# A three-stage decoder layer on one core: both norms' moments on ScalarE, two context products on VectorE

## The chip, the cores and the metric

The kernel runs on one core of a Trainium2 chip. The metric is the device time of one launch in microseconds (us). In what follows PE is TensorE (its weight loads are listed apart, as PEld), DVE is VectorE, ACT is ScalarE, POOL is GpSimd and SP is SyncE.

## The reference

A post-norm decoder layer works on `x` of 16 sequences of 256 tokens with 512 channels. Each of its three parts is added to its input and followed by a norm without parameters.

```python
def reference(x, ctx_2048, w_q, w_k, w_v, w_o, ssm_kernel, D, gamma, W):
    x = _layernorm(x + attention(x, w_q, w_k, w_v, w_o))       # 16 heads, causal, ternary weights
    x = _layernorm(x + _xattn(ctx_2048, ctx_2048, x, ssm_kernel, D, 8))
    x = _layernorm(x + _ffn(x, gamma, W))
    return x

def _layernorm(x, eps=1e-05):
    return (x - mean(x)) / sqrt(var(x) + eps)                  # over the 512 channels

def _xattn(k, v, q, ssm_kernel, D, head_dim):                  # 32 heads of 8 rows, length 512
    kv = einsum('bhil,bhjl->bijhl', k, v)                      # products of rows i and j
    y = causal_convolution(kv, ssm_kernel)                     # along l, by FFT
    return einsum('bijhl,bhil->bjhl', y + kv * D, q)

def _ffn(x, gamma, W):
    xn = x * rsqrt(mean(x * x) + 1e-6) * gamma
    a = 127 / (max(abs(xn)) + 1e-5)                            # 8-bit rounding per token
    return einsum('bsd,od->bso', clip(round(xn * a), -128, 127) / a, ternary(W))
```

Since the context is both `k` and `v`, the product of rows i and j is that of j and i. The second norm's output is fed to the feed-forward part, whose sum is normed a third time.

## The kernel before

The attention stage fills the first half of the time and leaves its normed result transposed in SBUF (`x1t`). The change lies in the second stage, which goes over the 32 heads of the convolution layer; one head is one 128-token tile of the output (8 rows times 16 sequences), so a head carries the convolution, both norms and the feed-forward part of those tokens. The heads are pipelined: step `h` of the loop does the convolution of head `h`, the second norm of head `h-1`, the feed-forward product of head `h-2`, and the third norm's output of head `h-3`. An instruction's place in each engine's queue is the place of its call in the loop, since all five engines are scheduled by hand.

For a head, `kv` (128 x 4 blocks x 576) holds the context products: five groups of columns, by the distance 0 to 4 between the two rows multiplied. The squares (distance 0) come from ACT (L760), the groups 1, 2 and 3 (512 elements per partition each) and 4 (256 elements) from POOL (L754, `multiply`). The convolution is a matrix product with a Toeplitz tile `w`: `multiplied` (L785) makes block `lb` of 4 from `lb+1` blocks of `kv` into `y`, of which there are two buffers in PSUM. In the profile, blocks 0, 1, 2 and 3 show up as 4, 8, 12 and 16 matmuls; they are called y0 to y3 below.

`with_queries` (L797, L800, L803, L809, L812, all DVE) multiplies `y` by the queries `q` into `own` and `turn`; its last instruction, L812, frees the `y` buffer. `add` (POOL, L960, and L962 for blocks 1 to 3) sums them, and `read` (PE, L820) transposes and accumulates them into `tok`, 128 tokens by 512 channels. `tok` is complete when block 3 of the head has been read, which happens in the next step.

The second norm: `second_moments` takes the mean and variance of `tok` (DVE bn_stats L835, bn_aggr L837, and quarters of the variance for two roots, L840), ACT takes the root (L845), DVE its reciprocal (L851), ACT a Newton step (L855), DVE the reciprocal of that (L863). `second_centred` (L878) makes `xn`, `second_max` (L882) its maximum, and `second_norm` the normed rows `x2` (ACT, L888), the small scales (DVE, L890 to L895) and the rounded activations `fq_t` and `fq_i` (ACT, L897 and L188). SP transposes these by DMA, PE multiplies (L907, `acc_f`), and `feed_forward` makes `r3 = acc_f * inv + x2` (DVE, L911) and the third norm's moments, again by L835, L837 and L840. `finish` writes the result a step later (ACT L926, then a DMA). `copy` (ACT, L772 and L773) fetches the next head's queries from `x1t`.

After the loop, `last_heads` finishes the last three heads; nothing is left there to overlap with, and its instructions keep the order of the calls. The last head's activations are transposed by PE and copied by ACT (`fit`, L196).

Four lines of the first stage are used later for comparison: L158 (DVE) compares weights, with two inputs in SBUF; L132 (ACT) sums absolute weights with the accumulator; L182 scales activations (there on POOL) and L251 (POOL) builds a diagonal.

## Time and profile before

| | us |
|---|---|
| median of 3 runs (lowest to highest) | 863.07 (862.62 to 864.34) |
| the profiled execution, its whole time | 861.76 |
| its span, first to last instruction | 860.0 |
| busy in the span: PE / DVE / ACT / POOL | 803.8 / 690.5 / 427.0 / 583.4 |
| busy in one step of the second stage, 682.08 to 694.48 (12.40 us): PE / DVE / ACT / POOL | 12.25 / 10.85 / 5.22 / 11.52 |

The profile is of one execution, 1.3 us under the median. The second stage begins at about 441 us with the first L785 and its steady steps end at about 841 us. All times of instructions below are us from the start of the span.

### The profile page before, as it was taken

The numbers are of one execution on the slowest core, as the hardware profiler recorded it, in microseconds if no ns is written. First come the engines' busy times: TensorE is split into PE (matmuls) and PEld (weight loads), VectorE is DVE, ScalarE is ACT, GpSimd is POOL, SyncE is SP. The second block draws the span as 40 slices with busy tenths as digits, with TensorE's granted clock in tenths as the row PEclk, the third lists the DMA queues.
The fourth block names the chain that finished last, engine by engine and source line by source line (L and its number), as shares of the span: only waits on it lengthen the run. The fifth ranks groups of instructions, "written<-read, shape, count | busy, mean of one in ns | idle before, by whom it ended". The sixth has DMA issues, their size and how long they took to land.

```text
span 860.0 us, 20228 instructions
## 1 busy us (share of the span) xinstructions
PE 803.8 (93%) x7754; PEld 555.9 (65%) x7754; DVE 690.5 (80%) x1889; ACT 427.0 (50%) x707; POOL 583.4 (68%) x652
## 2 busy tenths in 40 slices
PE   4889999999999999998878999999999999999993
PEld 3556666666666666665646767776777677777762
DVE  6757887788888778876666888988898889888885
ACT  6555655556565555655644334433443444344434
POOL 5265544545454454544639999999999999999980
PEclk9999999999999999999979999999999999999997
DMA  9111222333122222211320233223323332333211
GB/s 319 45 33 53 66 69 69 75 76 76 26 63 68 71 75 76 51 39 35 88 65 19 69 99 95 71 81 99 88 67 91 99 84 68 95 98 74 75 38 55
DMA packets 102207, 64.51 MB, mean 75 GB/s; under 512 B 66464, under 2 KB 83104, under 8 KB 102112
## 3 DMA queue, kind: packets, MB, share of 16 engines
q1 hardware_dynamic: 102112, 63.23, 27.5%
q8 instruction: 61, 1.00, 0.5%
q14 instruction: 34, 0.28, 0.1%
HBM read 43.34 MB, written 8.47 MB: 60 GB/s over the span
## 4 chain that ended last, share of the span: by engine, by line
PE 77%; DVE 10%; ACT 6%; issue 4%; POOL 2%; DMA 0%; ACTq 0%; DVEq 0%; POOLq 0%
PE y L785 32%; PE s L341 6%; PE acc L293 6%; PE s L381 5%; ACT p L386 4%; PE tok L820 4%; PE pv L409 4%; PE s L334 4%; PE acc_o L482 3%; DVE nmax L346 3%; PE acc_f L907 3%; PE sums L416 2%; PE s L374 2%; PE acc_v L311 2%; PE tp L528 1%
## 5 line engine op out<-in xcount | busy, mean ns | idle before, releaser
L785 PE MATMUL y<-kv,w 128*128 128x288 f32 x1280 | 335.0, 409 | 4.4 <-DVE turn L812 2.0
L785 PEld LDWEIGHTS y<-kv,w 128*128 128x128 f32 x1280 | 234.0, 191 | 64.9 <-PE tok L820 10.5
L960 POOL TENSOR_TENSOR own<-own,turn 128x512 f32<-128x512 f32 x127 | 161.7, 1274 | 21.1 <-DVE turn L812 11.0
L390 POOL TENSOR_SCALAR_AFFINE_SELECT p<-p 128x512 f32<-128x512 f32 x128 | 81.3, 659 | 139.5 <-ACT p L386 129.1
L754 POOL TENSOR_TENSOR kv<-c 128x512 f32<-128x512 f32 (+1 forms) x128 | 144.4, 1140 | 2.9 <-PE sums L416 2.9
L346 DVE TENSOR_REDUCE nmax<-s 128x4 f32<-128x512 f32 (+1 forms) x128 | 116.5, 952 | 35.5 <-PE s L341 35.5
L386 ACT ACTIVATE p<-s 128x1536 f32<-128x1536 f32 x64 | 92.9, 1452 | 70.3 <-PE s L381 70.2
L845 ACT ACTIVATE root<-quarter 128x3 f32<-128x3 f32 (+2 forms) x34 | 7.0, 204 | 159.5 <-DVE quarter L840 159.5
L396 POOL TENSOR_TENSOR both<-p 128x512 f32<-128x512 f32 x64 | 82.3, 1286 | 5.3
L797 DVE SCALAR_TENSOR_TENSOR own<-y,q 128x128 f32<-128x128 f32 x128 | 36.7, 286 | 50.5 <-PE y L785 42.6
L962 POOL TENSOR_TENSOR own<-own 128x256 f32<-128x256 f32 x95 | 69.1, 727 | 7.5
L293 PE MATMUL acc<-xit,w 128*128 128x256 bf16 x504 | 68.9, 276 | 3.6 <-DVE w L158 3.4
L800 DVE TENSOR_TENSOR own<-y,q 128x384 f32<-128x384 f32 x128 | 70.1, 548 | 0.0
L803 DVE TENSOR_TENSOR turn<-y,q 128x384 f32<-128x384 f32 x128 | 70.1, 548 | 0.0
L820 PEld LDWEIGHTS tok<-ident,own 128*128 128x128 f32 x318 | 37.7, 141 | 38.5 <-POOL own L962 26.0
L293 PEld LDWEIGHTS <-w 128*128 128x128 bf16 x512 | 45.9, 99 | 24.1 <-issue 8.5
L820 PE MATMUL tok<-ident,own 128*128 128x128 f32 x318 | 58.7, 283 | 2.4 <-issue 1.2
L341 PE MATMUL s<-kt,qt 32*128 32x128 f32 (+1 forms) x1024 | 60.0, 348 | 0.0
L381 PE MATMUL s<-qt,kt 32*128 32x256 f32 (+1 forms) x1024 | 57.4, 335 | 0.0
L409 PE MATMUL pv<-p,va 128*32 128x256 f32 (+1 forms) x1024 | 54.9, 332 | 0.0
L421 ACT COPY ot<-pv 128x256 f32<-128x256 f32 x64 | 23.9, 373 | 50.8 <-PE pv L409 50.2
L334 PE MATMUL s<-mask,ident_h 128*128 128x256 bf16 x256 | 38.3, 271 | 11.0 <-ACT p L386 9.9
(148 smaller groups left out, 1359.8 us busy)
## 6 DMA issues: line engine op xcount, KB each, us to landing
xt<-in_x SPq DMA_DIRECT2D x16, 512.0 KB, 4.1
xr<-in_x SPq DMA_DIRECT2D x16, 512.0 KB, 4.6
c<-in_ctx_t SPq DMA_DIRECT2D x32, 256.0 KB, 3.3
w<-taps SPq DMA_DIRECT2D x32, 256.0 KB, 4.1
out_y<-res SPq DMA_DIRECT2D x31, 256.0 KB, 2.3
c<-in_ctx_t SPq DMA_DIRECT2D x32, 128.0 KB, 3.2
x1t<-in_w_q SPq DMA_DIRECT2D x1, 1024.0 KB, 6.6
x1t<-in_w_k SPq DMA_DIRECT2D x1, 1024.0 KB, 9.4
```

The lines of the kernel that those rows point to most:

```text
L293: nc.tensor.matmul(acc[:, j, :], w[:, c, o * P : (o + 1) * P], m.xit[:, c].rearrange("p t k -> p (t k)"), start=(c == 0), stop=(c == NB - 1),)
L341: nc.tensor.matmul(s[:, r, lo:hi], m.qt[rows, g, q0 : q0 + P], m.kt[rows, g, 0:nk], start=False, stop=True, skip_group_check=True,)
L346: nc.vector.tensor_reduce(m.nmax[:, t, :, g], s[:, :, cols], AX.X, ALU.max, negate=True)
L381: nc.tensor.matmul(s[:, r, lo:hi], m.kt[rows, g, k0 : k0 + P], m.qt[rows, g, q0:S], start=False, stop=True, skip_group_check=True,)
L386: nc.scalar.activation(p, s[:, :, 0 : 3 * P], AF.Exp)
L390: nc.gpsimd.affine_select(out=own, in_=own, compare_op=ALU.is_ge, fill=0.0, base=0, pattern=[[0, 4], [1, P]], channel_multiplier=-1,)
L396: nc.gpsimd.tensor_tensor(both, p[:, :, P : 2 * P], p[:, :, 2 * P : 3 * P], ALU.add)
L409: nc.tensor.matmul(acc[rows, q0:S], m.va[:, j, 4 * g + r, :], p[:, r, src], start=(j == 0), stop=(j == 1), skip_group_check=True, tile_pos ...
L754: nc.gpsimd.tensor_tensor(kv[:, :, at : at + n * B].rearrange("p c (i b) -> p c i b", b=B), c[:, :, i : i + n, :], c[:, :, i + d : i + d + ...
L785: nc.tensor.matmul(y[:, Y0 + k * HALF : Y0 + (k + 1) * HALF], lhs, kv[:, mb, k * HALF : (k + 1) * HALF], start=(mb == 0), stop=(mb == lb),)
L820: nc.tensor.matmul(tok[:, lb, :], lhsT=own[:, d, :], rhs=ident, is_transpose=True, start=(d == last), stop=(d == 0))
L960: nc.gpsimd.tensor_tensor(own[:, 0:4, :], own[:, 0:4, :], turns[lb], ALU.add)
```

## The change

Four things are edited.

1. `moments2` takes the moments on ACT, for both the second and the third norm. One ACTIVATE Copy over 512 elements gives the sum by its accumulator, a small one scales it to minus the mean, an ACTIVATE Square with that as its bias gives the sum of squared deviations, and small ones (two for the second norm, one for the third) make the quarters. Their wide output goes to a tile that nobody reads.
2. The products of distance 3 and 4 move from POOL to DVE, to other places of the loop: distance 3 in front of `second_centred`, distance 4 between `copy` and `feed_forward`. For the first head, POOL still makes them, distance 4 now after distance 3.
3. `second_max` is called ahead of the Newton step instead of after it (in the loop only).
4. `x2` is made after `fq_i` instead of ahead of the small scales. The sign of the mean is flipped where it is used.

```diff
+        unused = pb.tile([P, E], BF16, name="unused")
...
-            def multiply(k):
-                part(k * P, XD, 0, k)
-                if k == 2:
-                    part(4 * P, 4, 0, 4)
+            def multiply(k, engine):
+                part(k * P, 4 if k == 4 else XD, 0, k, engine)
...
         def moments2(src, roots, forms):
-            st = sm.tile([P, 6], F32, name="st2")
-            nc.vector.bn_stats(st, src)
-            mv = sm.tile([P, 2], F32, name="mv2")
-            nc.vector.bn_aggr(mv, st)
+            total = sm.tile([P, 1], F32, name="total2")
+            nc.scalar.activation(unused, src, AF.Copy, accum_out=total)
+            minus_mean = sm.tile([P, 1], F32, name="minus_mean")
+            nc.scalar.activation(minus_mean, total, AF.Copy, scale=-1.0 / E)
+            squares = sm.tile([P, 1], F32, name="squares")
+            nc.scalar.activation(unused, src, AF.Square, bias=minus_mean, accum_out=squares)
             for i in forms:
                 a, b = FORMS[i]
-                nc.vector.tensor_scalar(roots.quarter[:, i : i + 1], mv[:, 1:2], a / 4, b / 4, ALU.mult, ALU.add)
-            return mv[:, 0:1]
+                nc.scalar.activation(
+                    roots.quarter[:, i : i + 1], squares, AF.Copy, scale=a / (4 * E), bias=b / 4
+                )
+            return minus_mean
...
         def second_norm(m, roots):
...
-            m.x2 = fp.tile([P, E], F32, name="x2")
-            nc.scalar.activation(m.x2, m.flat, AF.Identity, bias=shift, scale=rstd)
...
             m.fi = rounded(fp, "fq", m.ft)
+            m.x2 = fp.tile([P, E], F32, name="x2")
+            nc.scalar.activation(m.x2, m.flat, AF.Identity, bias=shift, scale=rstd)
...
             multiply(first_head, 3)
+            multiply(first_head, 4)
...
+                on(multiply, h + 1, 3, nc.vector)
                 on(second_centred, h - 1)
+                on(second_max, h - 1)
                 if h > 0:
                     newton(roots)
-                on(second_max, h - 1)
...
-                on(multiply, h + 1, 3)
                 on(second_norm, h - 1, roots)
                 on(turn, h - 1)
                 on(finish, h - 3, roots, h - 3)
                 on(copy, h + 1)
+                on(multiply, h + 1, 4, nc.vector)
                 on(feed_forward, h - 2, ahead)
```

More of the change, by code (lines that the diff above doesn't have):

```diff
@@ L751, in prepare, with part @@
             kv = cp.tile([P, NB, NPAIR], F32, name="kv")
-            def part(at, n, i, d):
-                nc.gpsimd.tensor_tensor(
+            def part(at, n, i, d, engine):
+                engine.tensor_tensor(
                     kv[:, :, at : at + n * B].rearrange("p c (i b) -> p c i b", b=B),
@@ L866, in shifted @@
             shift = sm.tile([P, 1], F32, name="shift")
-            nc.vector.tensor_scalar(shift, mean, res, -1.0, ALU.mult, ALU.mult)
+            nc.vector.tensor_scalar(shift, mean, res, None, ALU.mult)
             return shift
@@ L877, in second_centred @@
             m.xn = fp.tile([P, E], F32, name="xn")
-            nc.vector.scalar_tensor_tensor(m.xn, m.flat, m.mean, gam, ALU.subtract, ALU.mult)
+            nc.vector.scalar_tensor_tensor(m.xn, m.flat, m.mean, gam, ALU.add, ALU.mult)
         def second_max(m):
@@ L940, in square, with multiply @@
             m.inputs[5]()
-        def multiply(m, k):
-            m.inputs[3](k)
+        def multiply(m, k, engine=nc.gpsimd):
+            m.inputs[3](k, engine)
         def copy(m, *blocks):
```

## The prediction

> **What bounds the kernel now.** The page comes first: PE is busy 803.8 of 860.0 us, and the only lines touched by the change run in the second stage. The table of windows for one of its steps, 682.08 to 694.48, has PE busy 12.25 of 12.40 us, POOL 11.52, DVE 10.85, ACT 5.22. Three engines look full, so shares decide nothing; the chain of waits in order of time does. One step of it:

> ```profile
> 682.08 2.18 PE y L785 x8
> 684.26 0.39 PE tok L820 x2
> 684.65 2.91 PE y L785 x12
> 687.57 0.86 PE acc_f L907 x4
> 688.43 0.44 PE tok L820 x4
> 688.87 3.90 PE y L785 x16
> ...
> 692.86 0.29 DVE own L797
> 693.15 0.47 DVE own L800
> ...
> 694.35 0.14 issue
> 694.48 2.18 PE y L785 x8
> ```

> The same picture repeats every 12.40 us (y1 starts at 632.48, 644.88, 657.28 and so on). The loop is: y3 ends at 692.76; 0.10 later DVE starts on it and needs 1.48 to free the buffer; 0.15 later PE starts y1, 1.72 after the end of y3; then 2.18 + 0.39 + 2.91 + 0.86 + 0.44 + 3.90 = 10.68 bring the next y3. 1.72 + 10.68 = 12.40. Two terms hold a stall: y1 takes 2.18 and not 8 x 0.243 = 1.94, since its weight load comes after the wait, and the pair of tok reads takes 0.39 and not 0.22, since it waits for POOL's sum of block 3, which itself starts 0.15 after DVE's L812.

> What DVE and POOL do just before that is in the timeline:

> ```profile
> 690.53 1.28 POOL L754 TENSOR_TENSOR kv<-c 128x512 f32<-128x512 f32 x1
> 690.75 0.74 DVE L911 SCALAR_TENSOR_TENSOR r<-acc_f,inv,x 128x512 f32<-128x512 f32 x1
> 691.53 0.69 DVE L835 BATCH_NORM_STATS2 st<-r 128x6 f32<-128x512 f32 x1
> 691.75 1.28 POOL L960 TENSOR_TENSOR own<-own,turn 128x512 f32<-128x512 f32 x1
> 692.86 0.29 DVE L797 SCALAR_TENSOR_TENSOR own<-y,q 128x128 f32<-128x128 f32 x1 [0.23 <-PE y L785]
> ```

> Whether DVE is ever late for y3 is in the list of waits (484 to 840 us; who waited for whom, in total, times, longest). L797 is the one that waits:

> ```profile
> DVE own L797 <- PE y L785: 35.3, 55, 1.0
> ```

> DVE has 0.23 us to spare before y3 and POOL 0.64 before its sum of block 3. So relieving either moves nothing in the loop; making DVE late by more than its slack costs each step the difference.

> **Part by part, in the loop.** *DVE, removed:* second moments 685.77 to 686.84, 1.07 us; third moments 691.53 to 692.62, 1.09. *DVE, added:* two tensor_tensor. L800 (384 elements) takes 548 ns and L809 (64) 215, so 1.04 ns an element: 0.68 for distance 3 (data phase 0.53) and 0.42 for distance 4 (0.27). Net 1.06 less. *POOL, removed:* 1.28 + 0.73 (L754's two forms) = 2.01 us.

> *The wait that is added.* These two are the first DVE instructions of this stage with both inputs in SBUF; all others with two tensor inputs read one of them from PSUM. The first stage shows what such an instruction does beside POOL:

> ```profile
> L158 DVE SCALAR_TENSOR_TENSOR w<-x1t,limits x2: 1285/1437/1589, 11.5 to 17.0; 128x1024 bf16<-128x1024 f32 x2
> L251 POOL TENSOR_SCALAR diag<-ident,x_v x4: 602/616/1562, 7.8 to 19.0; 128x128 f32<-128x128 f32 x4
> ```

> Alone it took 1285 ns. At 16.95 it found POOL's L182 running until 17.48, and took 1589: 0.53 of waiting and then 1.06 of data. The POOL instruction queued behind it took 1562 instead of 616. So I take it that DVE waits for the end of the running POOL instruction, runs its data phase, and POOL's next one waits for that. [...]

> Distance 3: issued at 685.77 behind block 1, it finds POOL's L960 (685.35 to 686.62), and ends at 686.62 + 0.53 = 687.15 or so. Behind it on DVE queue xn, its maximum, the reciprocal L851 and block 2; who waits for these are ACT's Newton step, POOL's sum of block 2 and the `y` buffer of the next y0. xn 687.1 to 687.8, maximum to 688.55, L851 at 688.47, block 2 from 688.56 instead of 688.22 to 690.04. The buffer is wanted at 692.76, so 2.7 us cover that. POOL, held until 687.17, ends distance 2 at 688.3, the sum of block 1 at 690.3, and the first half of the sum of block 2 (L960) at 691.55, where before it only began at 691.75.

> Distance 4: before, r3 was issued 1.14 after L863; now L863 is at 689.96, so distance 4 is issued at 691.10, waits for L960 until 691.55, and ends at 691.83; r3 ends at 692.49. y3 is due at 692.86: slack 0.37 instead of 0.23. PE's y0 (692.98) now waits for this product too, with 1.1 us to spare. So the loop is not touched: 0.

> *ACT, added per step.* Rows: 128x512 with constants 0.63 (L188), with one pointer 0.71 (L897), ACTIVATION_READ_ACCUMULATOR 190 ns (L132), of which 0.10 overlaps, a small one 0.20 (L845), a dependent step 0.03. Sum, minus mean, squares and a quarter: 0.63 + 0.09 + 0.03 + 0.20 + 0.03 + 0.71 + 0.09 + 0.03 + 0.20 = 2.01, a second quarter 0.10: 4.1 a step, 9.3 busy of 12.40. Its order: fq_t at 690.98, fq_i, x2, result, both copies to 694.56, third moments, squares to 697.0. tok is complete at 697.05, so the second moments start at once at 697.10, and the root ends at 699.44, which in the step shown is 687.04. DVE asks for it at 688.47. Slack 1.4 us, cost 0; the minus mean (685.65) is there before xn (687.1). The copies end 0.9 later than before, so DVE's L800 of block 0 starts near 694.60 instead of 694.45; DVE then idles 1.04 before y1's result, so 0. SP's transpose goes 0.2 later (its product is 7 us away) and the output DMA 0.9 later, with it the next head's loads, wanted two steps on. 0. x2 is read a step later, 0. Swapping the maximum and the Newton step is within the slack just used.

> A second price on ACT is excluded by the trace: L760 (Square) and the copies already alternate with the root, and ACT_TABLE_LOAD occurs once in this stage (1283 ns, at 464.49). [...]

> **At the ends.** Start: in step h=1, PE's read of block 2 stood 0.81 us for POOL (471.23), behind an L754 of distance 3 that goes; that step took 12.70 against 12.40, so -0.3. The first head's reordered products end at 437.9 on POOL, y0 begins at 441.30: 0.

> The tail is in the open, and here the moments are a chain:

> ```profile
> 849.15 0.80 ACT L926 ACTIVATE res<-r,shift,res 128x512 f32<-128x512 f32 x1
> 849.94 0.59 ACT L196 COPY fit<-tp 128x512 bf16<-128x512 bf16 x1
> 850.58 1.89 PE L907 MATMUL acc_f<-w,fit 128*128 128x512 bf16 x4 [0.68 <-ACT fit L196]
> 853.30 0.69 DVE L835 BATCH_NORM_STATS2 st<-r 128x6 f32<-128x512 f32 x1
> 854.43 0.20 ACT L845 ACTIVATE root<-quarter 128x1 f32<-128x1 f32 x1 [1.89 <-DVE quarter L840]
> ```

> (a) Last head's second moments: tok complete at 843.73; root ended at 845.16, now 843.77 + 2.01 + 0.10 + 0.23 = 846.11. DVE's L851 had waited behind xn, so the Newton step ends 0.66 later (847.30); fq_t no longer waits for x2 and starts at 848.37 instead of 847.87: +0.50, fq_i ends at 849.75. (b) The copy of `fit` stands in ACT's queue behind the early result and behind `feed_forward` of the head before, whose moments are now ACT's too, and x2 is there as well: x2 849.66 to 850.44, result to 851.15, moments 851.06 to 853.07, copy at 852.98 instead of 849.94: +3.04, which contains (a). (c) The last third moments: r3's end to root's end 853.26 to 854.63 = 1.37, now 0.03 + 2.01 + 0.23 = 2.27: +0.9. Tail: +3.9.

> Sum: 0 - 0.3 + 3.9 = +3.6. The profiled execution's 861.76 becomes 865.4; it lies 1.3 under the median, so 863.07 becomes 866.7. Unknown sizes: each of the six accumulator reads on the tail's path may hide wholly or not at all (0 to 0.19, near the row's 0.09: together -0.5 to +0.6); ACT and DVE read tok together in the tail (a collision is in no row: 0 to one xn, 0.74; I take 0). The case alone: 865 to 868.5.

> **Rivals.**

> *Distance 4 misses its gap.* If it is issued after 691.55, it meets POOL's second half, L962 (to 692.4), ends at 692.64, r3 at 693.30, and block 3 is 0.44 late. In 29 steps +12.8 with the tail +16.4: 879.5. It decides from 0.45 us of extra delay on DVE between L812 and r3. [...] Against: the measured wait of L158 was exact to 0.01. Chance 0.12.

> *PE gains from the relief.* With POOL 2 us freer the pair of tok reads might lose its 0.17 stall and y1 its 0.24: 0.41 x 29 = -11.9, with the ends 854.8. For it: PE's reads waited 23.4 us for L962 by the list of waits. Against: both hang on L812, which comes 1.58 after y3 whatever DVE did before. Chance 0.08.

> *A cheap tail.* If the moments of the last-but-one head don't hold up the copy of `fit`, only (a) and (c) remain: +1.1, 864.2. Against: the queue keeps the order of the calls. Chance 0.12.

> **How the numbers follow.** The forecast has 0.68. About 0.2% (1.7 us) can be told from no change: faster is the second rival, 0.08; same is the third and a sliver of the forecast, 0.13; slower the rest, 0.79. The range, 863.0 to 871.0, holds forecast and cheap tail and a mild form of the first rival (a delay of up to 0.15 a step, 4.4 us), and leaves out the strong form and the second rival.

> **What would show it.** Right: steps still of 12.40; DVE idle before L797 of block 3 of about 0.4; L754 on DVE longer than 0.68 by the wait (near 1.4 for distance 3, 0.87 for distance 4); POOL idle for over 2 us a step; `fit` copied 11.4 us after the last y3 instead of 8.4. Wrong: steps of another length, or L797 of block 3 waiting for r3 instead of y3.

## The result, and the profile after

The changed kernel takes 866.65 us (median of 19 runs, 864.78 to 869.7) against 863.74 (861.15 to 865.81) for the kernel before on the same chip. The ratio is 1.0042 with a 95% interval of 1.003 to 1.0053: slower by 3.6 us (2.6 to 4.6), more than the 0.2% that can be told from no change. (The two medians are 2.9 apart, the means of the 19 runs 3.6.) The forecast was 866.7 and slower.

The page shows work that moved, with nothing gained where it counts. ACT has 121.5 us more than before (427.0), POOL 43.6 less (583.4), DVE 1.7 more (690.5):

```profile
PE 799.2 (92%) x7754; PEld 558.8 (65%) x7754; DVE 692.2 (80%) x1727; ACT 548.5 (63%) x1123; POOL 539.8 (62%) x590
```

The line numbers have shifted: the `y` matmul is L784 now, the five lines of `block` L796 to L811, the reads of `tok` L819, the products L755, POOL's two sums L964 and L966, r3 L915. The chain of waits in order of time, for PE's part of one step (start, length, engine and line):

```profile
695.39 2.18 PE y L784 x8
697.57 0.39 PE tok L819 x2
697.96 2.91 PE y L784 x12
700.87 0.88 PE acc_f L911 x4
...
707.79 2.18 PE y L784 x8
```

From y1 to y1 it is 707.79 - 695.39 = 12.40, as before, and the two stalls are still there: y1 takes 2.18, the pair of reads 0.39. Measured from one end of y3 to the next, the 29 steps from h=2 on take 12.39 to 12.40 in both kernels, but for one of 12.45 before, and the step h=1 takes 12.40 now and took 12.70.

The timeline of the same stretch has the two new products on DVE, and POOL around them (start, length, engine and line; in brackets the idle time before it and what ended that):

```profile
695.39 1.28 POOL L964 TENSOR_TENSOR own<-own,turn 128x512 f32<-128x512 f32 x1 [2.04 <-DVE turn L811]
...
698.65 1.27 POOL L964 TENSOR_TENSOR own<-own,turn 128x512 f32<-128x512 f32 x1
699.08 1.39 DVE L755 TENSOR_TENSOR kv<-c 128x512 f32<-128x512 f32 x1
699.88 1.73 POOL L755 TENSOR_TENSOR kv<-c 128x512 f32<-128x512 f32 x1
700.09 0.20 ACT L849 ACTIVATE root<-quarter 128x3 f32<-128x3 f32 x1
701.77 0.16 DVE L855 RECIPROCAL inv_root<-root 128x3 f32<-128x3 f32 x1
703.59 1.27 POOL L964 TENSOR_TENSOR own<-own,turn 128x512 f32<-128x512 f32 x1
704.36 0.79 DVE L755 TENSOR_TENSOR kv<-c 128x256 f32<-128x256 f32 x1
705.07 0.74 DVE L915 SCALAR_TENSOR_TENSOR r<-acc_f,inv,x 128x512 f32<-128x512 f32 x1
706.16 0.29 DVE L796 SCALAR_TENSOR_TENSOR own<-y,q 128x128 f32<-128x128 f32 x1 [0.35 <-PE y L784]
```

Distance 3 is issued at 699.08 while POOL runs L964 until 699.92, and ends at 700.47, 0.55 after that. Distance 4 finds L964 running until 704.86 and ends at 705.15, 0.29 after. POOL's own product, queued behind distance 3, takes 1.73 where 1.28 is usual. None of it arrives anywhere: DVE still idles 0.35 before block 3 and is released by y3, the root has been there for 1.48 when DVE asks for it, and POOL idles for 2.04 in each step, waiting for DVE's L811. The list of waits (484 to 840 us; who waited for whom, in total, times, longest) says the same for all steps:

```profile
POOL own L964 <- DVE turn L811: 59.6, 30, 2.1
DVE own L796 <- PE y L784: 36.6, 57, 1.0
```

So the loss lies in the tail. From the end of the last y3 (842.44; before 841.55) to the end of the span it takes 22.4 us and took 18.5, +3.9. The timeline of ACT there:

```profile
849.28 0.72 ACT L899 ACTIVATE fq_t<-xn,mul 128x512 f32<-128x512 f32 x1 [1.06 <-DVE mul L895]
...
851.24 0.80 ACT L930 ACTIVATE res<-r,shift,res 128x512 f32<-128x512 f32 x1
851.94 0.62 ACT L835 ACTIVATE unused<-r 128x512 bf16<-128x512 f32 x1
...
853.76 0.20 ACT L842 ACTIVATE quarter<-squares 128x1 f32<-128x1 f32 x1
853.87 0.57 ACT L196 COPY fit<-tp 128x512 bf16<-128x512 bf16 x1
...
857.20 0.63 ACT L835 ACTIVATE unused<-r 128x512 bf16<-128x512 f32 x1 [0.75 <-DVE r L915]
...
859.27 0.20 ACT L849 ACTIVATE root<-quarter 128x1 f32<-128x1 f32 x1
```

The copy of `fit` (L196), which the last feed-forward product needs, starts 11.43 after the last y3 (before 8.39): it stands behind the early result (L930) and behind the third moments of the head before (851.94 to 853.96). Then the last moments take 2.30 from r3 to the root's end, and took 1.37.

The two profiled spans, 864.86 and 860.05, differ by 4.8. That is 3.9 of the tail, less 0.4 in the steps (0.3 of it in h=1), and 1.28 by which the first y3 ends later (459.11, before 457.83). The last is no work of the change: in this execution PE's full clock was granted from 22.08 us on, in that of before from 16.25 (16 matmuls of L293 take 3.60 from 18.51 on here, and 1.92 from 18.60 on there). In the experiments it comes out either way whatever the kernel; the fifth below, which begins as the changed kernel does, had it from 16.41 on, and there the first y3 ends at 457.83, as before.

### The profile page after: what moved, and what is told of

It is laid out like the page before. It is cut to its first block, busy times and chain, and to the rows that moved or that the text cites. A ratio compares the mean times of both kernels' runs of the same rounds, so it can differ in the third digit from the quotient of the medians.

```text
span 864.9 us, 20450 instructions
## 1 busy us (share of the span) xinstructions
PE 799.2 (92%) x7754; PEld 558.8 (65%) x7754; DVE 692.2 (80%) x1727; ACT 548.5 (63%) x1123; POOL 539.8 (62%) x590
## 4 chain that ended last, share of the span: by engine, by line
PE 61%; ACT 16%; DVE 15%; issue 6%; POOL 1%; DMA 0%; ACTq 0%; DVEq 0%; POOLq 0%
PE y L784 18%; PE s L341 6%; PE acc L293 6%; PE s L381 5%; ACT p L386 4%; PE pv L409 4%; PE s L334 4%; DVE nmax L346 3%; PE acc_o L482 3%; PE acc_f L911 3%; ACT x L902 3%; ACT fq_t L899 3%; ACT res L930 2%; PE sums L416 2%; PE s L374 2%
## 5 line engine op out<-in xcount | busy, mean ns | idle before, releaser
L784 PE MATMUL y<-kv,w 128*128 128x288 f32 x1280 | 334.9, 409 | 10.0 <-DVE turn L811 10.0
L784 PEld LDWEIGHTS y<-kv,w 128*128 128x128 f32 x1280 | 233.7, 190 | 70.6 <-PE tok L819 16.5
L964 POOL TENSOR_TENSOR own<-own,turn 128x512 f32<-128x512 f32 x127 | 162.1, 1277 | 63.7 <-DVE turn L811 62.2
L755 POOL TENSOR_TENSOR kv<-c 128x512 f32<-128x512 f32 x66 | 97.3, 1475 | 2.9 <-PE sums L416 2.9
L396 POOL TENSOR_TENSOR both<-p 128x512 f32<-128x512 f32 x64 | 82.2, 1285 | 5.3
L796 DVE SCALAR_TENSOR_TENSOR own<-y,q 128x128 f32<-128x128 f32 x128 | 36.4, 284 | 49.7 <-PE y L784 43.2
L966 POOL TENSOR_TENSOR own<-own 128x256 f32<-128x256 f32 x95 | 70.9, 746 | 7.4
L293 PE MATMUL acc<-xit,w 128*128 128x256 bf16 x504 | 70.6, 281 | 3.2 <-DVE w L158 3.0
L755 DVE TENSOR_TENSOR kv<-c 128x512 f32<-128x512 f32 (+1 forms) x62 | 68.2, 1100 | 0.0
L859 ACT ACTIVATE full<-quarter,root,inv_root 128x1 f32<-128x1 f32 x96 | 30.4, 377 | 51.1 <-DVE inv_root L855 51.1
L293 PEld LDWEIGHTS <-w 128*128 128x128 bf16 x512 | 46.8, 101 | 24.7 <-issue 8.5
L819 PEld LDWEIGHTS tok<-ident,own 128*128 128x128 f32 x318 | 40.1, 141 | 29.6 <-POOL own L966 12.5
L819 PE MATMUL tok<-ident,own 128*128 128x128 f32 x318 | 57.1, 278 | 1.2 <-POOL own L964 1.2
```

The costliest lines, as they stand in the source:

```text
L293: nc.tensor.matmul(acc[:, j, :], w[:, c, o * P : (o + 1) * P], m.xit[:, c].rearrange("p t k -> p (t k)"), start=(c == 0), stop=(c == NB - 1),)
L396: nc.gpsimd.tensor_tensor(both, p[:, :, P : 2 * P], p[:, :, 2 * P : 3 * P], ALU.add)
L755: engine.tensor_tensor(kv[:, :, at : at + n * B].rearrange("p c (i b) -> p c i b", b=B), c[:, :, i : i + n, :], c[:, :, i + d : i + d + n, ...
L784: nc.tensor.matmul(y[:, Y0 + k * HALF : Y0 + (k + 1) * HALF], lhs, kv[:, mb, k * HALF : (k + 1) * HALF], start=(mb == 0), stop=(mb == lb),)
L819: nc.tensor.matmul(tok[:, lb, :], lhsT=own[:, d, :], rhs=ident, is_transpose=True, start=(d == last), stop=(d == 0))
L964: nc.gpsimd.tensor_tensor(own[:, 0:4, :], own[:, 0:4, :], turns[lb], ALU.add)
```

## The experiments

The theory: the loop is worth nothing in either direction, since PE's own order sets it, and the whole loss is the moments in the tail. Rivals: the products on DVE cost something in the loop, or the relief of POOL and DVE gains something that the tail gives back twice. Ratios are against runs of the kernel before on the same chip.

**Only the tail undone.** The last head's second moments and the last two heads' third moments go back to DVE (the old code as `moments_dve`); the loop stays as changed.

```diff
-            m.mean = moments2(m.flat, roots, (1, 2))
+            m.plus2 = m is heads[XH - 1]
+            m.mean = (moments_dve if m.plus2 else moments2)(m.flat, roots, (1, 2))
...
-            m.mean3 = moments2(m.r3, roots, (0,))
+            m.plus3 = m in heads[XH - 2 :]
+            m.mean3 = (moments_dve if m.plus3 else moments2)(m.r3, roots, (0,))
```

> The changed kernel with the moments of the last head's second norm and of the last two heads' third norm on VectorE again, as before the change; the loop is the changed one. My theory (the loop costs nothing, the loss is the tail): the copy of fit starts about 8.9 us after the end of the last y3 (8.4 before the change, 11.4 with it), the last r3 to its root takes 1.4 instead of 2.3, so 3.5 us less than the changed kernel and within 0.5 us of the kernel before; steps stay at 12.40. Rival (the loop or the start of the second stage pays for the busier ScalarE): it stays 2 us or more above the kernel before.

Measured: 864.38 against 864.62, ratio 0.9996 (0.9981 to 1.001), steps of 12.40. The timeline of its tail:

```profile
850.12 0.80 ACT L947 ACTIVATE res<-r,shift,res 128x512 f32<-128x512 f32 x1
850.83 0.57 ACT L196 COPY fit<-tp 128x512 bf16<-128x512 bf16 x1
...
855.30 0.20 ACT L849 ACTIVATE root<-quarter 128x1 f32<-128x1 f32 x1 [1.89 <-DVE quarter L884]
```

The copy follows the early result (L947 here) at once, 8.81 after the last y3, and the tail is 18.7 again. With the tail undone the loss is gone, with all of the loop's part still in.

**Only the order in the tail.** The last head's `fit` is copied ahead of `feed_forward` of the head before, so that the copy no longer stands behind that head's moments.

```diff
-            feed_forward(prev, one)
...   (the transpose and the copy into last.fit)
+            feed_forward(prev, one)
```

> The changed kernel, with the transposition of the last head's activations and the copy of fit called ahead of feed_forward of the head before; all else as changed. My theory: of the tail's 4 us, 1.9 are the copy of fit standing behind the last-but-one head's moments in ScalarE's queue, so 1.9 us less than the changed kernel, 1.7 above the kernel before. Rival (the chain of the last head's own moments is what costs): no gain, 3.6 above the kernel before.

Measured: 867.12, ratio 1.0029 (1.0016 to 1.0042). By the time alone this can't be told from the change's 1.0042; the trace tells them apart. The copy came 1.93 earlier, as expected, but the tail shrank by 0.70 only (21.7), not by 1.9. Its timeline:

```profile
854.62 0.57 ACT L196 COPY fit<-tp 128x512 bf16<-128x512 bf16 x1
855.24 1.89 PE L911 MATMUL acc_f<-w,fit 128*128 128x512 bf16 x4 [1.23 <-ACT fit L196]
857.39 0.17 DVE L855 RECIPROCAL inv_root<-root 128x1 f32<-128x1 f32 x1 [4.56 <-ACT root L849]
858.21 0.21 DVE L871 TENSOR_SCALAR shift<-minus_mean,res 128x1 f32<-128x1 f32 x1
858.34 0.74 DVE L915 SCALAR_TENSOR_TENSOR r<-acc_f,inv,x 128x512 f32<-128x512 f32 x1
```

PE has the last product done at 857.13, but r3 (L915) starts at 858.34. It stands on DVE's queue behind the Newton step of the head before (L855, L871), and that waits for ACT's moments of that head, which now come after the copy. The moments had only changed the place at which they hold up the tail.

**The products back on POOL.** Distances 3 and 4 return to the places that they had before; the moments stay on ACT.

```diff
+                on(multiply, h + 1, 4)
...
-                on(multiply, h + 1, 3, nc.vector)
...
+                on(multiply, h + 1, 3)
...
-                on(multiply, h + 1, 4, nc.vector)
```

> The changed kernel with the products of distance 3 and 4 on GpSimd again, in the places that they had before; the moments stay on ScalarE. My theory (GpSimd's relief is worth nothing in the loop, since y1 waits for VectorE's release of y3 either way): steps of 12.40, as the changed kernel, up to 0.3 us more for the step h=1. Rival (GpSimd's relief is what paid for other costs of the change): steps longer by 0.1 us or more, 3 us or more above the changed kernel.

Measured: 867.98, ratio 1.0036 (1.0024 to 1.0049). Steps of 12.40 (one of 12.59), and h=1 takes 12.69 again. PE's weight loads wait 23.5 us for POOL's second half again (23.4 before the change, 11.8 with it), yet the steps aren't longer for it. So two microseconds of POOL in each step are worth some 0.5 us in all: 0.3 in the step that the forecast named and 0.2 in one other.

**The moments back on DVE.** All moments return to DVE while both products stay there: the change's second half without its first.

```diff
-            m.mean = moments2(m.flat, roots, (1, 2))
+            m.mean = moments_dve(m.flat, roots, (1, 2))
...
-            m.mean3 = moments2(m.r3, roots, (0,))
+            m.mean3 = moments_dve(m.r3, roots, (0,))
```

> The changed kernel with all moments on VectorE again; the products of distance 3 and 4 stay on VectorE too. My theory (each of the two products waits for the GpSimd instruction that runs, and VectorE has about 0.3 us to spare): distance 3 now meets the product of distance 2, distance 4 the sum of block 2, r3 and its moments end 1.8 us after y3, so steps of about 14.2 and some 50 us more. Rival (no wait for GpSimd, only the 1.1 us of two more instructions): r3's moments end 0.75 us late, steps of 13.15, some 22 us more.

Measured: 925.19, ratio 1.0702 (1.0682 to 1.0722), +60.6. The first steps are 14.17, 14.17 and 14.18, as worked out, but after them steps of 15.69 alternate with steps of 12.7 to 13.9; the 29 steps from h=2 on are 14.45 in the mean. The timeline of PE at one such place, and the table of windows of two steps, one at 517 and this one (in the second: stretch, length, busy time of PE, PEld, DVE, ACT and POOL with counts, granted clock, DMA share, GB/s):

```profile
705.84 3.03 PE L784 MATMUL y<-kv,w 128*128 128x288 f32 x8 [2.12 <-DVE turn L811]
```

```profile
515.87:519.28 3.41, 1.62 (x7) 1.34 (x8) 3.00 (x12) 1.79 (x4) 1.54 (x2) 1.00 0.63 178
519.28:522.70 3.42, 3.42 (x16) 2.47 (x15) 2.69 (x10) 0.17 (x1) 3.42 (x4) 1.00 0.49 130
703.60:707.01 3.41, 1.29 (x7) 0.99 (x6) 3.34 (x13) 2.23 (x5) 1.17 (x1) 1.00 0.49 134
707.01:710.43 3.42, 3.42 (x10) 2.42 (x9) 1.52 (x7) 0.00 (x0) 3.34 (x5) 0.50 0.60 175
```

PE stands for 2.12 us waiting for DVE's L811; 1.2 us after it has started again its clock is 0.50 for 3.41 us. The steps have 13 such stretches. With steps of 14.17 the loss would be 1.77 x 29 = 51, with the mean of 14.45 it is 2.05 x 29 = 59, so the excess lies in the steps with these stretches.

**A second product of distance 4.** It is issued twice in a row on DVE, everything else as changed. This measures the wait of a DVE instruction with two inputs in SBUF for the running POOL instruction, and the point at which DVE's lateness begins to count.

```diff
                 on(multiply, h + 1, 4, nc.vector)
+                on(multiply, h + 1, 4, nc.vector)
```

> The changed kernel with the product of distance 4 issued twice in a row on VectorE (the same values are written twice). My theory (a VectorE instruction with both inputs in SBUF waits for the GpSimd instruction that runs): the second one meets the second half of GpSimd's sum of block 2, which the trace of the changed kernel has running until 705.74, ends 0.27 later, and r3 ends at 706.67 where block 3 started at 706.16: 0.43 to 0.5 late, steps of 12.85, 12 to 15 us above the changed kernel. Rival (VectorE pays only its own 0.34 us more): r3 ends at 706.15, in time, steps of 12.40, no difference.

Measured: 879.14, ratio 1.0173 (1.0156 to 1.019), steps of 12.83. First the groups of line L755 on DVE (least, median and most ns), then the timeline of DVE:

```profile
L755 DVE TENSOR_TENSOR kv<-c x93: 779/834/1410, 450.5 to 840.6; 128x256 f32<-128x256 f32 x62, 128x512 f32<-128x512 f32 x31
```

```profile
698.57 1.66 DVE L755 TENSOR_TENSOR kv<-c 128x256 f32<-128x256 f32 x2
700.15 0.74 DVE L915 SCALAR_TENSOR_TENSOR r<-acc_f,inv,x 128x512 f32<-128x512 f32 x1
700.81 0.28 DVE L796 SCALAR_TENSOR_TENSOR own<-y,q 128x128 f32<-128x128 f32 x1
```

Each of the 62 takes at least 779 ns where the prediction's estimate from L800 and L809 is 0.42 us without a wait, 0.27 of it data phase: the second of a pair waits for POOL's second half (699.16 to 699.95), as the forecast's first rival had it. L796 of block 3 has no idle before it any more, and each step pays 0.43. The rows also show what the wait costs: the rest of the POOL instruction that is running, here until 699.95, after which the pair ends 0.28 later, at 700.23.

**PE's order, first step.** If PE's order sets the loop, moving PE's own instructions must shorten it where relief of the others did not. With the tail undone as in the first experiment, the feed-forward product of two heads back is placed ahead of the reads of block 3, so that PE has something to do while POOL makes that sum.

```diff
+                on(feed_product, h - 2)
                 on(read, h - 1, 3)
...
                 on(block, h, 2)
-                on(feed_product, h - 2)
```

> The kernel of the first run (changed loop, tail's moments on VectorE), with the feed-forward product of PE called ahead of the read of block 3 instead of behind y2. My theory (the read of block 3 takes 0.39 instead of 0.22 since it waits for GpSimd, and any other PE work fills that wait): steps of 12.23, 29 times 0.17 or 5 us less than that kernel and than the kernel before. Rival (the 0.39 is the read's own cost): steps of 12.40, no gain.

Measured: 859.56, ratio 0.9941 (0.9929 to 0.9954). From y1 to y1 in its chain of waits 12.23, 0.17 less, which is the stall of the pair of reads:

```profile
695.26 2.19 PE y L784 x8
...
707.49 2.19 PE y L784 x8
```

**PE's order, second step.** The reads of block 0 go a step later, between y0 and y1 (`own` gets a fifth buffer), which gives DVE time to free the buffer of y1. Distance 4 goes back to POOL.

```diff
                 on(read, h - 1, 2)
+                on(read, h - 1, 0)
...
+                on(multiply, h + 1, 4)
...
-                on(read, h, 0)
...
-                on(multiply, h + 1, 4, nc.vector)
```

> The kernel of the first run, with three moves: the feed-forward product ahead of the read of block 3; the read of block 0 a step later, between y0 and y1 of the next head (own has 5 buffers for that); distance 4 on GpSimd again, in its place of before. My theory (the loop is the hand-over of y3 to VectorE and back, 1.72 us, in which PE has 1.41 us of other work): with 1.85 us of other work PE never waits and a step is its own work, 11.68 to 11.75; 29 times 0.65 to 0.72, 19 to 21 us below the kernel before (ratio 0.976 to 0.978). Rival (VectorE or ScalarE is the next bound at once, by r3 or by the copies of the queries): steps of 12.0 or more, at most 12 us below.

Measured: 841.36, ratio 0.9735 (0.9716 to 0.9753), 23 us faster than the kernel before, where 19 to 21 were expected; 29 steps of 0.68 less are 19.7, and the rest stays open. Its chain of waits is PE and nothing else:

```profile
688.37 6.79 PE y L784 x28
695.16 0.22 PE tok L819 x2
695.38 0.97 PE y L784 x4
696.35 0.68 PE tok L819 x6
697.03 1.97 PE y L784 x8
...
700.09 6.79 PE y L784 x28
```

The pair of reads takes 0.22 and y1 1.97: both stalls are gone, and a step takes 11.72.

**The same order in the kernel before.** Only these two moves of PE's instructions, on the kernel before: DVE keeps the moments, POOL the products.

```diff
+                on(read, h - 1, 0)
...
+                on(feed_product, h - 2)
                 on(read, h - 1, 3)
...
-                on(feed_product, h - 2)
...
-                on(read, h, 0)
```

> The kernel before, with two of these moves alone: the feed-forward product ahead of the read of block 3, the read of block 0 a step later. My theory (here VectorE needs 4.4 us from block 2 to the end of the third moments, so it becomes the bound, and GpSimd is full at 11.8): steps of 12.2 to 12.3, 3 to 6 us below the kernel before. So the relief of VectorE and GpSimd that the change brings would be worth 13 us or more once PE's order is loosened. Rival (the relief is worth nothing there either): steps as in the run with all moves, some 20 us below the kernel before.

Measured: 861.08, ratio 0.9948 (0.9935 to 0.9962), steps of 12.24 and 12.44 in turn. In the timeline of DVE block 3 now begins right behind the third moments, with no idle:

```profile
696.30 0.15 DVE L840 TENSOR_SCALAR quarter<-mv 128x1 f32<-128x1 f32 x1
696.37 0.28 DVE L797 SCALAR_TENSOR_TENSOR own<-y,q 128x128 f32<-128x128 f32 x1
```

PE's order is worth up to 0.68 a step (12.40 to 11.72), and here DVE and POOL allow 0.06 of it in the mean. That makes 1.7 us in 29 steps where the ratio says 4.5 and the medians 3.4. The profiled execution was the longest of its seven runs (864.53, mean granted clock 0.984); five of the others were granted 0.989, the runs of the kernel before 0.983 to 0.987. So part of the difference may be the clock and not the order; that isn't shown. The version at 841.36, measured beside this one, has the same order of PE and also the moments on ACT (but for the tail) and distance 3 on DVE: with PE's order loosened, that relief is worth 19.7 us.

**The same order in the changed kernel.** The same two moves alone on the changed kernel, tail included.

> The changed kernel as it is (all moments on ScalarE, tail included, distances 3 and 4 on VectorE) with the two moves in PE's order alone; beside e8, which has the same moves on the kernel before, it gives what the change is worth when PE's own order no longer sets the step. In e7, with distance 4 on GpSimd, r3 ended at 695.04, block 3 began at 695.20 after 0.16 of idle, and the buffer that it frees was wanted about 0.2 after it was free. Distance 4 on VectorE waits for the end of GpSimd's sum of block 2 (about 694.55 once GpSimd has lost that product) and ends 0.27 later, so that r3 ends near 695.56 and block 3 is late by about 0.3, y1 by about 0.1: steps of 11.8 (11.72 to 12.0). With the dear tail (3.9 over e7) the time is 841.4 + 0.1 x 29 + 3.9 = 848 (845 to 853), 13 us under e8 and 16 under the kernel before. Rival theory, the relief of VectorE and GpSimd by this change is worth nothing even then, because distance 4 takes back what the moments gave: steps of 12.3 as in e8, 861 + 3.9 = 865.

Measured: 854.26, ratio 0.9889 (0.9863 to 0.9916): 9.6 us faster than before, not 16. The steps are 11.95, inside what was given, but the tail is 23.7 us, and that is 5.1 and not 3.9 more than the 18.6 of the version at 841.36. The chain of waits of one step:

```profile
697.95 0.22 PE tok L819 x2
698.17 0.97 PE y L784 x4
699.14 0.67 PE tok L819 x6
699.81 0.04 issue
699.85 2.18 PE y L784 x8
...
709.90 0.22 PE tok L819 x2
```

y1 waits for 0.04 only, but it waits, and takes 2.18 and not 1.97: 0.25 a step, of which the expectation had 0.1. The 1.2 us in the tail are a wait on ACT's queue that the tail of the changed kernel didn't have. The timeline there:

```profile
831.16 0.66 PE L979 MATMUL tok<-ident,turn 128*128 128x128 f32 x4
833.18 0.58 ACT L835 ACTIVATE unused<-tok 128x512 bf16<-128x512 f32 x1
```

The last `tok` is complete at 831.82, and its moments begin 1.36 later, behind the third moments of the head before (in the changed kernel 0.03 later, 844.62 to 844.65).

This pair of runs answers what the change is for. In PE's old order it costs 0.42%; in the new order the ratio to the kernel before goes from 0.9948 to 0.9889, some 0.6% or 5 us better, with the dear tail still in it. The two were measured in different sessions, each beside its own runs of the kernel before, and with different granted clocks. The traces say the same without the start: from the end of the first y3 to the end of the span the change costs 3.5 us in the old order (405.8, before 402.2) and saves 8.1 in the new one (394.5 against 402.6).

## Why the prediction was right

- **The loop.** Cost forecast 0, measured 0: steps of 12.40 in both kernels, and the kernel with the tail undone has a ratio of 0.9996. The reason held too. Relieving POOL changed h=1 and one other step (third experiment), and only moving PE's instructions shortened the step (12.23, then 11.72). In the kernel before, the same moves gave 0.06 a step in the mean: there DVE and POOL are the next bound at once.
- **The products on DVE.** Distance 3 was put at the end of POOL's L960 plus 0.53, about 1.4; it takes 1.39. Distance 4 takes 0.79. The prediction has two values for it: its working gives 0.73 (691.10 to 691.83), its list of signs 0.87, which is the wait of 0.45 and the whole 0.42, not the data phase of 0.27 alone. The rule of the working held: L964 runs for 0.50 more when the product is issued, and the product ends 0.29 after that. The slack before block 3 is 0.35 (forecast 0.37). All of this came from two rows of the first stage.
- **ACT.** 4.1 a step was forecast; 121.5 over 32 heads is 3.8. The root's slack was given as 1.4 and is 1.48.
- **The start of the loop.** -0.3 in h=1, measured 12.70 to 12.40.
- **The tail.** (a) fq_t +0.50: it starts 6.84 after the last y3 and did 6.32 after it, +0.52. (b) The copy of `fit` +3.04: 8.39 to 11.43, +3.04. (c) r3 to root +0.9: 1.37 to 2.30, +0.93. Sum 3.9, measured 3.9. The two experiments on the tail show that the moments are its cause; they also show that (b) can't be won back by moving the copy alone: that gives 0.7, since the moments then hold up the tail in DVE's queue.
- **The total.** That the median came out 0.05 from the forecast is luck in part. The forecast added 3.6 to 863.07, the median of three runs; over 19 runs the kernel before is at 863.74 and the medians are 2.9 apart. The better test is the traces, in which tail and steps together give 3.9 - 0.4 = 3.5.
- **The rivals.** "Distance 4 misses its gap" did not come about, but its price is right: with the product doubled, 0.43 a step where 0.44 was given. "PE gains from the relief" did not either: y1 still takes 2.18 and the pair of reads 0.39, though PE's weight loads wait less for POOL's second half (11.8 us, before 23.4). "A cheap tail" fell with (b).
- **What went wrong behind it.** Moving the copy alone was expected to give 1.9 and gave 0.7, because only ACT's queue had been followed and not DVE's. The kernel with all moments on DVE cost 60.6 instead of some 50, since the clock had been taken as full throughout. The last experiment missed by 6 us: 0.15 in each of 29 steps (4.4, the dearer y1 after a wait) and 1.2 in the tail, again ACT's queue.

## What to carry to other kernels

Before moving work between engines, write down the loop that sets the step and ask which of its terms the move touches; here the two engines that were relieved were late only as followers of PE's own order, and 2 us less on POOL moved next to nothing. Then price the same move in the tail, where nothing covers it, and follow every queue there, not only that of the engine that got the work. And if relief is worth nothing, look for the instruction order that makes it worth something: the change lost 0.4% in the old order of PE and gained 0.6% in the new one.

## What the runs showed of the hardware

- The products on DVE (L755), with both inputs in SBUF, waited for the end of the POOL instruction that was running, and POOL's next one for them: 1.39 for 128x512 and 0.79 for 128x256, where the prediction's estimate from L800 and L809 is 0.68 and 0.42 without the wait, and 1.73 instead of 1.28 on POOL.
- A gap of 2.12 us on PE was followed by 3.41 us at a clock of 0.50 in the kernel with all moments on DVE, and there were 13 such stretches in its steps. The gap at 703.72, which fell whole into one window of the grid, was followed by one; the gap of 2.11 at 515.55, of which 1.79 lay in one window, was not. In the traces of the kernels before and after, the windows at full clock in which PE was idle for 2.13 us or more were followed by one at 0.50 (idle 2.93 from 432.68 and 3.41 from 845.69 before, 2.13 from 435.09 and 2.62 from 844.69 after), and those with 1.84 or less were not.
- A wait ahead of y1's first weight load made the group of eight take 2.18 instead of 1.97 at full clock, whether it was 0.04 us (last experiment), 0.15 (before), 0.33 (after) or 2.11 (all moments on DVE, at 517.66).
